# LayerNorm, S4 convolution and an NF4 gated MLP on one core: a rewritten head order, a smaller S4 transform, and the convolution's last chunk as one native matmul

## The chip, the core and the metric

The kernel runs on one core of a Trainium2 chip. The core has five engines, each with its own in-order queue: TensorE (PE in the profile; PEld is its weight load), VectorE (DVE), ScalarE (ACT), GpSimd (POOL) and SyncE (SP), which here only issues DMA transfers. The engines meet through semaphores. TensorE writes only to PSUM, the accumulator memory; the other data lie in SBUF, the on-chip memory of 128 partitions, or in DRAM. The metric is device time in microseconds (us) of one execution; lower is better.

## The reference

Input is x, four sequences of 512 rows by 512 columns, 2,048 rows in all. With xn = LayerNorm(x) over the columns, the output is

```
x + S4(xn) + MLP(xn)
S4(xn)  = causal convolution of each row of xn (512 long) with a kernel K of 512 taps, + D * xn
K       = ifft(at_roots).real, at_roots from a Cauchy sum over 64 states
MLP(xn) = (silu(xn Wg^T) * (xn Wu^T)) Wd^T,   Wg, Wu: 1792 x 512,   Wd: 512 x 1792
```

The three weights come as 4-bit codes (NF4, as int32 numbers 0 to 15) with a scale for every 64 numbers. All is float32.

## The kernel before

**Tiling.** The 2,048 rows are four blocks (tb 0 to 3) of 512; a block is four token tiles of 128 rows. The 1,792 hidden columns are 14 tiles m of 128; for each m the gate codes (k = 0) and the up codes (k = 1) form one matrix of 128 x 1024 numbers. A sum over 512 columns is four chunks of 128 (NC = 4).

**Matmuls.** Most products run as `fp32r` matmuls of three parts each: `split` and `part_of` make of a number a high part (h, on ACT), a low part (l, on DVE) and a part e (on DVE) that mends what the first two lose, with the factors LAM = 4096 and OUT = 4097. Three fp32r matmuls stand for one float32 product (`product`, L449; `conv`, L487; `down`, L514). The first matrix (m = 0) for blocks 0 and 1, the transposes, and the S4 setup use native float32 matmuls on unsplit numbers (`product_native`, L457). In the profile a native matmul makes two records, an fp32r one and a transpose make one.

**Dequantisation.** A code becomes its NF4 value by eight ACT steps in place (`bends`, L264), then DVE multiplies by the scales (`mul`, L599 in the head, L274 after it) and the parts are split off (`wp` tiles; L143 h, L145 l, L147 e).

**The head.** The string HEAD lists the work of the first three matrices and of the LayerNorm of all blocks, step by step: `stats.tb.j` (two DVE instructions for token tile j), `scale.tb.half` (two POOL instructions, add and power -0.5, for two token tiles), `norm.tb.j` (DVE), `turn.tb.half` (eight PE transposes), `copy` (ACT, turned rows to SBUF), `h`, `l`, `e` (parts of the turned rows), `bend.m.j.k.half` (bend j on 256 columns), `mul`, `w.m.part`, `native.k.tb.j.c` (two native matmuls for two token tiles and two chunks), `pass.k.m.tb.part` (four fp32r matmuls), `silu`, `gated`, and `awake.n` (n transposes of the identity, whose results nobody uses). After tracing the steps, dependencies are added that keep this order on ACT, DVE, PE and SP. GpSimd is not among them. Outside the head a scheduler orders each engine's queue by what is ready.

**After the head.** For m = 2 to 11 the loop dequantises matrix m + 1, runs `hidden` (all blocks; 24 matmuls of 128 x 512 for each), and at some m the weights of the down projection. `s4_roots` (after m = 2) forms the Cauchy sums: on PE four native matmuls into `pss` (L355), whose results DVE copies to `ss` (L360) and works on in small steps (L367 to L369). `s4_toeplitz` (after m = 3) forms K: 16 DVE steps make 128 x 128 tiles `ar` and `ai` for four residues r4, 12 native matmuls form `pm` (L421), and DVE and POOL make the Toeplitz matrix `toep`, split into `tp`. The convolution `conv(tb)` runs after m = 5 to 8: for each of four token tiles, column chunk i of the turned rows (i = 0 to 3) multiplies the first 512 - 128 i columns of `tp`, in three parts, so the matmuls are 512, 384, 256 and 128 wide. At the end `down` multiplies with Wd and adds, for each block.

Of the kernel before, what the change touches and what calls it, by code (L numbers as in the profile page):

```python
# [63 lines left out]


HEAD = """
awake.45 stats.0.0 bend.0.0.0.0 bend.0.0.0.1 bend.0.1.0.0 stats.0.1 bend.0.1.0.1
bend.0.2.0.0 stats.0.2 bend.0.2.0.1 scale.0.0 bend.0.3.0.0 bend.0.4.0.0 bend.0.3.0.1
stats.0.3 bend.0.5.0.0 bend.0.6.0.0 bend.0.4.0.1 norm.0.0 scale.0.1 bend.0.7.0.0 norm.0.1
bend.0.0.1.1 bend.0.5.0.1 mul.0.0.0 turn.0.0 awake.4 bend.0.1.1.1 norm.0.2 bend.0.6.0.1  # L70
norm.0.3 bend.0.0.1.0 bend.0.7.0.1 stats.1.0 turn.0.1 copy.0.0 mul.0.0.1 stats.1.1
bend.0.1.1.0 native.0.0.0.0 bend.0.2.1.1 bend.0.2.1.0 stats.1.3 scale.1.0 native.0.0.0.1
copy.0.1 stats.1.2 bend.0.3.1.0 native.0.0.1.0 bend.0.3.1.1 norm.1.0 scale.1.1 bend.0.4.1.0
native.0.0.1.1 bend.0.4.1.1 norm.1.1 bend.0.5.1.0 bend.0.5.1.1 norm.1.3 turn.1.0
bend.0.6.1.0 norm.1.2 bend.0.7.1.0 bend.0.6.1.1 turn.1.1 mul.0.1.0 bend.0.7.1.1 copy.1.0
mul.0.1.1 native.1.0.0.0 stats.2.0 w.0.0 native.1.0.0.1 stats.2.1 native.1.0.1.0 copy.1.1
stats.2.3 scale.2.0 native.1.1.0.0 bend.1.0 stats.2.2 native.1.0.1.1 norm.2.1 scale.2.1
silu.0.0 native.0.1.0.0 norm.2.0 bend.1.1 gated.0.0 turn.2.0 norm.2.3 norm.2.2
native.0.1.0.1 h.2.0 w.0.1 turn.2.1 bend.1.2 stats.3.0 native.0.1.1.0 bend.1.3 e.2.0
native.1.1.1.0 h.2.1 native.1.1.0.1 l.2.0 bend.1.4 native.0.1.1.1 l.2.1 native.1.1.1.1  # L80
bend.1.5 pass.1.0.2.0 e.2.1 bend.1.6 pass.1.0.2.1 w.0.2 bend.1.7 pass.0.0.2.0 silu.0.1 mul.1
pass.0.0.2.1 bend.2.0 pass.0.0.2.2 stats.3.1 w.1.0 pass.1.0.2.2 stats.3.3 scale.3.0 h.1
pass.0.1.2.0 w.1.1 pass.1.1.2.0 stats.3.2 silu.0.2 pass.0.1.2.1 norm.3.1 h.0 scale.3.1
pass.0.1.1.0 norm.3.0 gated.0.1 pass.1.1.2.1 w.1.2 bend.2.1 turn.3.0 norm.3.3 pass.1.1.2.2
h.3.0 gated.0.2 pass.0.1.2.2 norm.3.2 l.3.0 pass.1.1.1.0 silu.1.2 bend.2.2 turn.3.1
gated.1.2 load.3.0 e.3.0 pass.0.1.0.0 h.3.1 pass.1.1.0.0 bend.2.3 l.1 pass.0.1.3.0 bend.2.4
pass.1.1.3.0 bend.2.5 l.3.1 pass.0.1.1.1 bend.2.6 pass.1.1.1.1 e.3.1 pass.0.1.3.1 l.0
pass.0.0.3.0 pass.0.0.3.1 pass.0.1.3.2 e.1 pass.1.1.3.1 pass.0.0.3.2 e.0 pass.1.1.3.2
silu.0.3 bend.2.7 pass.1.0.3.0 silu.1.3 pass.1.1.1.2 mul.2 pass.1.1.0.1 gated.1.3 w.2.0
pass.0.1.0.1 w.2.1 pass.0.1.1.2 pass.1.1.0.2 silu.1.1 w.2.2 pass.0.1.0.2 gated.1.1  # L90
pass.0.2.0.0 silu.1.0 pass.1.2.0.0 pass.0.2.0.1 pass.1.2.0.1 pass.1.2.0.2 pass.0.2.0.2
pass.1.0.3.1 silu.2.0 pass.1.0.3.2 gated.0.3 gated.2.0 gated.1.0
"""


# [1 line left out]
def layernorm_s4_nf4_glu_kernel(  # L97
# [301 lines left out]
    def s4_toeplitz():  # L399
        qr, qi, nqi = roots["qr"], roots["qi"], roots["nqi"]  # L400
        b, b1 = (work.tile([P, 4, 512], F32, tag="xt", name=f"s4b{k}") for k in range(2))
        nc.sync.dma_start(b[:, 0:4, 0:256], dft)
        nc.sync.dma_start(b1[:, 0:2, :], twist)

        G.tensor_scalar(b[:, 0:4, 256:512], b[:, 0:4, 0:256], -1.0, None, ALU.mult)
        al, be, ar, ai = (b1[:, j, :] for j in range(4))
        for r4 in range(4):
            c = bass.ts(r4, P)
            o = slice(r4, r4 + 1)
            V.tensor_scalar(ar[:, c], al[:, c], qr[:, o], None, ALU.mult)  # L410
# [4 lines left out]

        pm = bank2("pm")[:, 0, :].rearrange("p (k q) -> p k q", k=4)
        for k, terms in enumerate((((0, 0),), ((2, 0),), ((1, 0), (3, 0)), ((1, 1), (3, 3)))):
            n = 2 * len(terms)
            for i, (r4, turn) in enumerate(terms):
                for part, lhsT in enumerate((ar, ai)):  # L420
                    T.matmul(  # L421
                        pm[:, k, :], lhsT[:, bass.ts(r4, P)],
                        b[:, r4, bass.ts((turn + part) % 4, P)],
                        start=(i == 0 and part == 0), stop=(2 * i + part == n - 1),
                    )
# [50 lines left out]
        gated(m, tb, ps[:, 1, :], silu(m, tb, ps[:, 0, :], OUT), OUT)  # L476


    def conv(tb, toep):
        xr = work.tile([P, 4, HD], F32, tag="xt", name=f"xr{tb}")  # L480
        nc.sync.dma_start(xr, rows(x, tb))
        for jj in range(0, 4, 2):
            po = bank2(f"pc{tb}_{jj}")
            for k in range(2):
                for i in range(NC):
                    for part in range(3):
                        T.matmul(  # L487
                            po[:, k, i * P : HD], xT[tb][part][:, jj + k, i, :],
                            toep[:, part, 0 : HD - i * P],
                            start=(i == 0 and part == 0), stop=(i == NC - 1 and part == 2),  # L490
                        )
# [252 lines left out]
```

## Time and profile before

| | us |
|---|---|
| median of 3 runs | 519.51 (519.39 to 519.62) |
| the profiled execution, its own time | 519.46 |
| its span, from first to last instruction | 517.7 |
| PE busy | 510.5 (99% of the span) |
| ACT busy | 261.6 (51%) |
| DVE busy | 260.3 (50%) |
| POOL busy | 22.1 (4%) |

The profile is one execution. Busy time of PE counts modelled ends of pipelined matmuls, so the distance between starts tells what a matmul takes from its queue. A line of the timeline has start, length, engine, source line, operation, written tile <- read tiles, shapes, count, and in brackets the idle time of the engine before it and what ended it. A line of the chain of waits in order of time has start, length, and what was waited for or ran. The view by windows gives TensorE a granted clock of 1.0 in every 2 us of the first 20; its own records begin at 5.2 us, and the `awake` transposes start every 0.213 us before that moment and every 0.109 us after it.

### The profile page before, as it was taken

How to read it: one execution, taken by the hardware profiler on the slowest of the kernel's cores; microseconds unless marked ns; L12 is line 12 of the kernel's file. 1: busy time of each engine (PE TensorE's matmuls, PEld its weight loads, DVE VectorE, ACT ScalarE, POOL GpSimd, SP SyncE). 2: the span in 40 equal slices, each digit the busy share in tenths (PEclk: the TensorE clock that was granted, in tenths of full speed). 3: DMA queues.
4: the chain of work that ended last, by engine and by line, in shares of the span. 5: the costliest groups of instructions: out<-in, count | busy, mean ns of one | idle time of the engine just before them, and what ended most of it. 6: DMA issues, size and time to landing. Idle time of an engine off the chain costs nothing.

```text
span 517.7 us, 6206 instructions
## 1 busy us (share of the span) xinstructions
PE 510.5 (99%) x2369; PEld 426.9 (82%) x2369; DVE 260.3 (50%) x352; ACT 261.6 (51%) x326; POOL 22.1 (4%) x42
## 2 busy tenths in 40 slices
PE   8999999999999999999999999999999999999996
PEld 7788888888888888888888888888888888888885
DVE  5899759935546553543522323113536536436412
ACT  7897369689999989899252202002112121121100
POOL 1310000200000000000000000121000000000000
PEclk9999999999999999999999999999999999999999
DMA  8915322796786678765845222789534524524102
GB/s 284 291 64 159 118 90 87 292 258 239 262 286 223 213 267 314 235 210 198 292 161 200 85 103 81 262 327 349 204 118 143 197 109 160 198 90 162 42 0 81
DMA packets 37085, 96.45 MB, mean 186 GB/s; under 512 B 4672, under 2 KB 5312, under 8 KB 34240
## 3 DMA queue, kind: packets, MB, share of 16 engines
q1 hardware_dynamic: 34320, 80.60, 44.9%
q0 software_dynamic: 2592, 15.21, 8.2%
q8 instruction: 18, 0.29, 0.2%
q10 hardware_dynamic: 144, 0.26, 0.1%
q14 instruction: 11, 0.09, 0.1%
HBM read 61.97 MB, written 34.08 MB: 186 GB/s over the span
## 4 chain that ended last, share of the span: by engine, by line
PE 96%; DMA 2%; SPq 1%; DVE 0%; issue 0%
PE gu L449 57%; PE po L514 30%; PE pc L487 6%; PE gu L457 2%; DMA sc_g1u<-in_gate_s_dram 2%; PE pt L204 1%; SPq L171 1%; PE pm L421 1%; SPq L250 0%; SPq L243 0%; PE pss L355 0%; DVE xo L521 0%; DVE x L192 0%
## 5 line engine op out<-in xcount | busy, mean ns | idle before, releaser
L514 PE MATMUL po<-wdt,hp 128*128 128x512 f32 x672 | 153.0, 390 | 0.0
L514 PEld LDWEIGHTS po<-wdt,hp 128*128 128x128 f32 x672 | 125.9, 188 | 27.0 <-DVE xo L521 0.9
L469 DVE SCALAR_TENSOR_TENSOR h<-gu,h 128x512 f32<-128x512 f32 x56 | 38.4, 688 | 109.4 <-ACT h L465 101.0
L143 ACT ACTIVATE hp<-hr 128x1024 fp32r<-128x1024 f32 x28 | 29.7, 1060 | 105.2 <-PE po L514 101.3
L465 ACT ACTIVATE h<-gu 128x512 f32<-128x512 f32 x56 | 33.0, 589 | 95.0 <-PE gu L449 95.0
L145 DVE TENSOR_TENSOR hp<-hr,hp 128x1024 fp32r<-128x1024 f32 x28 | 34.3, 1225 | 62.7 <-ACT hp L143 62.7
L147 DVE SCALAR_TENSOR_TENSOR hp<-hp 128x1024 fp32r<-128x1024 f32 x28 | 34.2, 1223 | 0.9
L449 PE MATMUL gu<-xhT,wp_gu 128*128 128x512 f32 x80 | 21.0, 394 | 0.0
L449 PE MATMUL gu<-xlT,wp_gu 128*128 128x512 f32 x80 | 20.7, 389 | 0.0
L487 PE MATMUL pc<-tp,xeT 128*128 128x512 f32 (+1 forms) x64 | 20.7, 323 | 0.0
L487 PE MATMUL pc<-tp,xlT 128*128 128x512 f32 (+1 forms) x64 | 20.6, 322 | 0.0
L449 PE MATMUL gu<-xeT,wp_gu 128*128 128x512 f32 x80 | 20.5, 390 | 0.0
L487 PE MATMUL pc<-tp,xhT 128*128 128x512 f32 (+1 forms) x64 | 20.3, 318 | 0.0
L521 DVE SCALAR_TENSOR_TENSOR xo<-po,xo 128x512 f32<-128x512 f32 x16 | 10.8, 688 | 18.1 <-PE po L514 18.1
L449 PEld LDWEIGHTS gu<-xlT,wp_gu 128*128 128x128 f32 x80 | 15.0, 188 | 3.1
L449 PEld LDWEIGHTS gu<-xhT,wp_gu 128*128 128x128 f32 x80 | 14.9, 188 | 3.2 <-ACT h L465 0.2
L449 PEld LDWEIGHTS gu<-xeT,wp_gu 128*128 128x128 f32 x80 | 14.9, 188 | 3.1
L457 PE MATMUL gu<-xf,q_g0u 128*128 128x256 f32 x64 | 14.6, 382 | 0.0
L457 PEld LDWEIGHTS gu<-xf,q_g0u 128*128 128x128 f32 x64 | 11.7, 190 | 1.8 <-DVE q_g0u L599 0.2
L487 PEld LDWEIGHTS pc<-tp,xhT 128*128 128x128 f32 x64 | 12.2, 190 | 0.9
L487 PEld LDWEIGHTS pc<-tp,xlT 128*128 128x128 f32 x64 | 12.0, 188 | 0.8
L487 PEld LDWEIGHTS pc<-tp,xeT 128*128 128x128 f32 x64 | 12.1, 188 | 0.6
(271 smaller groups left out, 912.1 us busy)
## 6 DMA issues: line engine op xcount, KB each, us to landing
hd<-h SPq DMA_DIRECT2D x56, 256.0 KB, 2.9
hr<-hd SPq DMA_DIRECT2D x28, 512.0 KB, 3.3
wdt<-wdd POOLq DMA_DIRECT2D x7, 1024.0 KB, 6.8
xr<-in_x_dram SPq DMA_DIRECT2D x4, 1024.0 KB, 6.8
rd<-xr SPq DMA_DIRECT2D x4, 1024.0 KB, 5.8
xo<-rd POOLq DMA_DIRECT2D x4, 1024.0 KB, 5.9
out_dram<-xo SPq DMA_DIRECT2D x16, 256.0 KB, 3.5
wdt<-wdd POOLq DMA_DIRECT2D x7, 512.0 KB, 7.3
```

Source lines behind the costliest of these rows:

```text
L143: S.activation(dst[0], src, AF.Copy, scale=TRIM)
L145: V.tensor_tensor(dst[1], src, f(dst[0]), ALU.subtract)
L147: V.scalar_tensor_tensor(dst[2], f(dst[1]), -LAM, f(dst[0]), ALU.mult, ALU.add)
L171: nc.sync.dma_start(xs[tb][:, j : j + step, :], rows(x, tb)[:, j : j + step, :])
L204: T.transpose(pt[:, i, bass.ts(c, P)], xs[tb][:, jj + i, bass.ts(c, P)], ident)
L449: T.matmul(ps[:, k, :], wp[:, part, k, bass.ts(c, P)], xT[tb][part][:, :, c, :], start=(part == 0 and c == 0), stop=(part == 2 and c == NC ...
L457: T.matmul(ps[:, k, j.start * P : j.stop * P], w[:, k, bass.ts(c, P)], xf[tb].rearrange("p j (c q) -> p j c q", c=NC)[:, j, c, :], start=( ...
L465: S.activation(h, pg, AF.Silu, scale=unit)
L469: V.scalar_tensor_tensor(h, pu, unit, h, ALU.mult, ALU.mult)
L487: T.matmul(po[:, k, i * P : HD], xT[tb][part][:, jj + k, i, :], toep[:, part, 0 : HD - i * P], start=(i == 0 and part == 0), stop=(i == NC ...
L514: T.matmul(po[j], hp[:, part, k, bass.ts(j, P)], wd(p, part, k), start=(p == 0 and k == 0 and part == 0), stop=(p == NPR - 1 and k == 1 an ...
L521: V.scalar_tensor_tensor(o, po[j], OUT, o, ALU.mult, ALU.add)
```

## The change

Three things are changed. First, HEAD is another list, and GpSimd is added to the engines on which it is kept. In the new list the code bends of the first matrix alternate between its two halves, `scale` steps stand directly behind their statistics, block 0 instead of block 1 is split first of these two, and the last steps of the three matrices stand in another order. The first lines of the list before:

```diff
-awake.45 stats.0.0 bend.0.0.0.0 bend.0.0.0.1 bend.0.1.0.0 stats.0.1 bend.0.1.0.1
-bend.0.2.0.0 stats.0.2 bend.0.2.0.1 scale.0.0 bend.0.3.0.0 bend.0.4.0.0 bend.0.3.0.1
-stats.0.3 bend.0.5.0.0 bend.0.6.0.0 bend.0.4.0.1 norm.0.0 scale.0.1 bend.0.7.0.0 norm.0.1
-bend.0.0.1.1 bend.0.5.0.1 mul.0.0.0 turn.0.0 awake.4 bend.0.1.1.1 norm.0.2 bend.0.6.0.1
-norm.0.3 bend.0.0.1.0 bend.0.7.0.1 stats.1.0 turn.0.1 copy.0.0 mul.0.0.1 stats.1.1
-bend.0.1.1.0 native.0.0.0.0 bend.0.2.1.1 bend.0.2.1.0 stats.1.3 scale.1.0 native.0.0.0.1
-copy.0.1 stats.1.2 bend.0.3.1.0 native.0.0.1.0 bend.0.3.1.1 norm.1.0 scale.1.1 bend.0.4.1.0
-native.0.0.1.1 bend.0.4.1.1 norm.1.1 bend.0.5.1.0 bend.0.5.1.1 norm.1.3 turn.1.0
-bend.0.6.1.0 norm.1.2 bend.0.7.1.0 bend.0.6.1.1 turn.1.1 mul.0.1.0 bend.0.7.1.1 copy.1.0
-mul.0.1.1 native.1.0.0.0 stats.2.0 w.0.0 native.1.0.0.1 stats.2.1 native.1.0.1.0 copy.1.1
...
-pass.0.1.0.1 w.2.1 pass.0.1.1.2 pass.1.1.0.2 silu.1.1 w.2.2 pass.0.1.0.2 gated.1.1
-pass.0.2.0.0 silu.1.0 pass.1.2.0.0 pass.0.2.0.1 pass.1.2.0.1 pass.1.2.0.2 pass.0.2.0.2
-pass.1.0.3.1 silu.2.0 pass.1.0.3.2 gated.0.3 gated.2.0 gated.1.0
```

and now:

```diff
+awake.43 stats.0.0 bend.0.0.0.0 bend.0.0.0.1 bend.0.1.0.0 stats.0.1 bend.0.1.0.1
+bend.0.2.0.0 bend.0.2.0.1 stats.0.2 scale.0.0 bend.0.3.0.0 bend.0.3.0.1 stats.0.3
+bend.0.4.0.0 bend.0.4.0.1 bend.0.5.0.0 norm.0.0 scale.0.1 bend.0.0.1.0 bend.0.5.0.1 norm.0.1
+bend.0.6.0.0 turn.0.0 awake.3 bend.0.6.0.1 norm.0.3 bend.0.1.1.0 bend.0.7.0.0 norm.0.2
+bend.0.7.0.1 stats.1.1 turn.0.1 copy.0.0 mul.0.0.0 bend.0.2.1.0 mul.0.0.1 native.0.0.0.0
+bend.0.0.1.1 stats.1.0 bend.0.3.1.0 copy.0.1 native.0.0.0.1 stats.1.3 scale.1.0 bend.0.4.1.0
+native.0.0.1.0 stats.1.2 bend.0.1.1.1 bend.0.5.1.0 bend.0.2.1.1 native.0.0.1.1 norm.1.1
+scale.1.1 bend.0.6.1.0 norm.1.0 bend.0.3.1.1 bend.0.7.1.0 turn.1.0 bend.0.4.1.1 mul.0.1.0
+bend.0.5.1.1 norm.1.3 native.1.0.0.0 bend.0.6.1.1 norm.1.2 bend.0.7.1.1 silu.0.0 turn.1.1
+mul.0.1.1 copy.1.0 native.1.0.1.0 stats.2.2 copy.1.1 stats.2.3 native.0.1.0.0 stats.2.0
...
+silu.1.3 pass.0.1.1.2 w.2.2 pass.1.1.1.2 gated.1.3 pass.1.0.3.1 pass.0.2.0.0 pass.0.0.3.2
+pass.0.2.0.1 silu.0.3 silu.1.1 pass.1.0.3.2 pass.1.2.0.0 gated.0.3 gated.1.1 pass.1.2.0.1
+pass.0.2.0.2 pass.1.2.0.2 silu.2.0 gated.2.0
```

Second, the S4 transform: the term of residue 3 is the mirrored conjugate of that of residue 1, so the host arranges the constants (`_layouts`) so that `s4_toeplitz` adds the fourth residue's `ar` and `ai` onto the second's, and `pm` needs eight matmuls; the cosine table loses a quarter.

Third, the last chunk of the convolution: `last_chunk(tb)` joins the high and low part of a block's last column chunk to whole float32 numbers in a buffer of its own (tag "xn", two buffers), `tn` holds the first 128 columns of `toep` divided by OUT, and one native matmul of 128 x 128 takes the place of three fp32r ones of that width.

```diff
ident = const.tile([P, P], F32, tag="ident", name="ident")
     make_identity(nc, ident)
     tp = const.tile([P, 3, L], F32R, tag="tp", name="tp")
+    tn = const.tile([P, P], F32, tag="tn", name="tn")
     const.tile([P, 16], F32, tag="fill", name="fill")
 
 
@@ -399,30 +401,38 @@
     def s4_toeplitz():
         qr, qi, nqi = roots["qr"], roots["qi"], roots["nqi"]
         b, b1 = (work.tile([P, 4, 512], F32, tag="xt", name=f"s4b{k}") for k in range(2))
-        nc.sync.dma_start(b[:, 0:4, 0:256], dft)
+        nc.sync.dma_start(b[:, 0:3, 0:256], dft)
         nc.sync.dma_start(b1[:, 0:2, :], twist)
 
-        G.tensor_scalar(b[:, 0:4, 256:512], b[:, 0:4, 0:256], -1.0, None, ALU.mult)
+        G.tensor_scalar(b[:, 0:3, 256:512], b[:, 0:3, 0:256], -1.0, None, ALU.mult)
         al, be, ar, ai = (b1[:, j, :] for j in range(4))
+
+
         for r4 in range(4):
+            to = bass.ts((0, 1, 2, 1)[r4], P)
             c = bass.ts(r4, P)
             o = slice(r4, r4 + 1)
-            V.tensor_scalar(ar[:, c], al[:, c], qr[:, o], None, ALU.mult)
-            V.scalar_tensor_tensor(ar[:, c], be[:, c], nqi[:, o], ar[:, c], ALU.mult, ALU.add)
-            V.tensor_scalar(ai[:, c], al[:, c], qi[:, o], None, ALU.mult)
-            V.scalar_tensor_tensor(ai[:, c], be[:, c], qr[:, o], ai[:, c], ALU.mult, ALU.add)
+            for dst, s1, s2 in (
+                ((ar, qr, nqi), (ai, qi, qr)) if r4 < 3 else ((ar, qr, qi), (ai, nqi, qr))
+            ):
+                if r4 < 3:
+                    V.tensor_scalar(dst[:, to], al[:, c], s1[:, o], None, ALU.mult)
+                else:
+                    V.scalar_tensor_tensor(
+                        dst[:, to], al[:, c], s1[:, o], dst[:, to], ALU.mult, ALU.add
+                    )
+                V.scalar_tensor_tensor(
+                    dst[:, to], be[:, c], s2[:, o], dst[:, to], ALU.mult, ALU.add
+                )
 
 
         pm = bank2("pm")[:, 0, :].rearrange("p (k q) -> p k q", k=4)
-        for k, terms in enumerate((((0, 0),), ((2, 0),), ((1, 0), (3, 0)), ((1, 1), (3, 3)))):
-            n = 2 * len(terms)
-            for i, (r4, turn) in enumerate(terms):
-                for part, lhsT in enumerate((ar, ai)):
-                    T.matmul(
-                        pm[:, k, :], lhsT[:, bass.ts(r4, P)],
-                        b[:, r4, bass.ts((turn + part) % 4, P)],
-                        start=(i == 0 and part == 0), stop=(2 * i + part == n - 1),
-                    )
+        for k, (r4, turn) in enumerate(((0, 0), (2, 0), (1, 0), (1, 1))):
+            for part, lhsT in enumerate((ar, ai)):
+                T.matmul(
+                    pm[:, k, :], lhsT[:, bass.ts(r4, P)], b[:, r4, bass.ts(turn + part, P)],
+                    start=(part == 0), stop=(part == 1),
+                )
         toep = work.tile([P, L], F32, tag="h", name="toep", bufs=4)
         tk = toep.rearrange("p (k q) -> p k q", k=4)
         cd = b1[:, 0, 0:384].rearrange("p (k q) -> p k q", k=3)
@@ -440,6 +450,7 @@
             toep[:, 0:P], ident, row[:, 64:65], toep[:, 0:P], ALU.mult, ALU.add
         )
         split([tp[:, i, :] for i in range(3)], toep)
+        S.activation(tn, toep[:, 0:P], AF.Copy, scale=1.0 / OUT)
         return tp
 
 
@@ -476,19 +487,32 @@
         gated(m, tb, ps[:, 1, :], silu(m, tb, ps[:, 0, :], OUT), OUT)
 
 
+
+
+    whole = {}
+
+    def last_chunk(tb):
+        whole[tb] = work.tile([P, 4, P], F32, tag="xn", name=f"xn{tb}")
+        h, low = (f(xT[tb][i][:, :, NC - 1, :]) for i in range(2))
+        V.scalar_tensor_tensor(whole[tb], h, LAM, low, ALU.mult, ALU.add)
+
     def conv(tb, toep):
         xr = work.tile([P, 4, HD], F32, tag="xt", name=f"xr{tb}")
         nc.sync.dma_start(xr, rows(x, tb))
         for jj in range(0, 4, 2):
             po = bank2(f"pc{tb}_{jj}")
             for k in range(2):
-                for i in range(NC):
+                for i in range(NC - 1):
                     for part in range(3):
                         T.matmul(
                             po[:, k, i * P : HD], xT[tb][part][:, jj + k, i, :],
                             toep[:, part, 0 : HD - i * P],
-                            start=(i == 0 and part == 0), stop=(i == NC - 1 and part == 2),
+                            start=(i == 0 and part == 0), stop=False,
                         )
+                T.matmul(
+                    po[:, k, (NC - 1) * P : HD], whole[tb][:, jj + k, :], tn,
+                    start=False, stop=True,
+                )
             o = xr[:, jj : jj + 2, :]
             V.scalar_tensor_tensor(o, po, OUT, o, ALU.mult, ALU.add)
         nc.sync.dma_start(res_dram[tb], xr)
@@ -628,13 +652,15 @@
         qs.pop(gu(m))
     last = {}
     order = mybir.DependencyInfo(mybir.DependencyClass.NoSync, mybir.DependencyReason.DATA)
-    ordered = (S.engine, V.engine, T.engine, sp.engine)
+    ordered = (S.engine, V.engine, T.engine, G.engine, sp.engine)
     end = len(traced)
     for ins in list(traced[start:end]):
         if ins.engine in last and ins.engine in ordered:
             tc.add_manual_dep(ins, last[ins.engine].name, order, reason="order of the first tiles")
         last[ins.engine] = ins
     for m in range(2, NMT - 2):
+        if 5 <= m < 9:
+            last_chunk(m - 5)
         wp[m + 1] = dequant(gu(m + 1))
         for tb in range(1 if m == 2 else 0, NTB):
             hidden(m, tb, wp[m])
@@ -699,9 +725,12 @@
     row = [np.asarray(a[f"L0_attn_{n}"]).reshape(-1) for n in ("Bp", "D", "log_step")]
 
     lr = 4 * np.arange(P)[:, None] + np.arange(4)[None, :]
+    lr[:, 3] = lr[::-1, 3]
     half = np.pi * lr / L
     th = 2 * np.pi * ((lr[:, :, None] * np.arange(P)) % L) / L
     tw = np.pi * ((lr[:, :, None] * (1 - 2 * np.arange(P))) % (2 * L)) / L
+    tw = np.stack([np.cos(tw), np.sin(tw)], axis=1) / L
+    tw[:, 1, 3] *= -1.0
     f = np.float32
     return {
         "x": np.asarray(a["L0_attn_u"]).reshape(NTOK, HD),
@@ -715,8 +744,8 @@
         "s4_row": np.concatenate(row)[None, :],
         "trig": np.stack([np.sin(half), np.cos(half)]).transpose(0, 2, 1).reshape(2, L).astype(f),
         "cos_col": np.cos(half).astype(f),
-        "dft": np.concatenate([np.cos(th), -np.sin(th)], axis=2).astype(f),
-        "twist": (np.stack([np.cos(tw), np.sin(tw)], axis=1) / L).reshape(P, 2, 512).astype(f),
+        "dft": np.concatenate([np.cos(th), -np.sin(th)], axis=2)[:, :3].astype(f),
+        "twist": tw.reshape(P, 2, 512).astype(f),
     }
```

More of the change, by code (lines that the diff above doesn't have):

```diff
@@ L73 @@
-copy.0.1 stats.1.2 bend.0.3.1.0 native.0.0.1.0 bend.0.3.1.1 norm.1.0 scale.1.1 bend.0.4.1.0
-native.0.0.1.1 bend.0.4.1.1 norm.1.1 bend.0.5.1.0 bend.0.5.1.1 norm.1.3 turn.1.0
-bend.0.6.1.0 norm.1.2 bend.0.7.1.0 bend.0.6.1.1 turn.1.1 mul.0.1.0 bend.0.7.1.1 copy.1.0
-mul.0.1.1 native.1.0.0.0 stats.2.0 w.0.0 native.1.0.0.1 stats.2.1 native.1.0.1.0 copy.1.1
-stats.2.3 scale.2.0 native.1.1.0.0 bend.1.0 stats.2.2 native.1.0.1.1 norm.2.1 scale.2.1
-silu.0.0 native.0.1.0.0 norm.2.0 bend.1.1 gated.0.0 turn.2.0 norm.2.3 norm.2.2
@@ L79 @@
[L79 to L89, printed above, removed]
-pass.0.1.0.1 w.2.1 pass.0.1.1.2 pass.1.1.0.2 silu.1.1 w.2.2 pass.0.1.0.2 gated.1.1
@@ new lines @@
+native.1.0.0.1 w.0.0 scale.2.1 stats.2.1 native.0.1.0.1 bend.1.0 norm.2.3 scale.2.0
+native.1.0.1.1 bend.1.1 w.0.1 native.1.1.0.0 bend.1.2 norm.2.0 native.0.1.1.0 norm.2.1
+bend.1.3 gated.0.0 turn.2.0 norm.2.2 native.1.1.0.1 h.2.0 w.0.2 turn.2.1 bend.1.4 e.2.0
+native.0.1.1.1 h.2.1 native.1.1.1.0 l.2.0 bend.1.5 native.1.1.1.1 stats.3.1 silu.0.1
+pass.1.0.2.0 l.2.1 bend.1.6 pass.0.0.2.0 bend.1.7 e.2.1 pass.0.0.2.1 pass.1.0.2.1 mul.1
+pass.0.0.2.2 stats.3.3 w.1.0 pass.1.0.2.2 stats.3.0 h.0 pass.0.1.2.0 w.1.1 scale.3.0
@@ new lines @@
+pass.1.1.2.0 gated.0.1 bend.2.0 pass.0.1.2.1 w.1.2 silu.0.2 pass.1.1.2.1 h.1 l.0
+pass.0.1.0.0 pass.1.1.0.0 bend.2.1 pass.1.1.2.2 stats.3.2 bend.2.2 pass.0.1.2.2 norm.3.1
+scale.3.1 norm.3.0 pass.0.1.0.1 silu.1.2 e.0 bend.2.3 pass.1.1.0.1 turn.3.0 norm.3.3
+pass.0.1.0.2 h.3.0 gated.0.2 pass.1.1.0.2 norm.3.2 gated.1.2 load.3.0 turn.3.1 silu.1.0
+e.3.0 pass.0.1.1.0 h.3.1 gated.1.0 pass.1.1.1.0 bend.2.4 l.3.0 pass.0.1.3.0 bend.2.5 l.3.1
+pass.1.1.3.0 bend.2.6 pass.0.0.3.0 e.3.1 bend.2.7 pass.0.1.3.1 l.1 pass.1.1.3.1 pass.1.0.3.0
@@ L93 @@
+pass.0.0.3.1 mul.2 pass.0.1.1.1 e.1 w.2.0 pass.0.1.3.2 pass.1.1.3.2 w.2.1 pass.1.1.1.1
+silu.1.3 pass.0.1.1.2 w.2.2 pass.1.1.1.2 gated.1.3 pass.1.0.3.1 pass.0.2.0.0 pass.0.0.3.2
+pass.0.2.0.1 silu.0.3 silu.1.1 pass.1.0.3.2 pass.1.2.0.0 gated.0.3 gated.1.1 pass.1.2.0.1
+pass.0.2.0.2 pass.1.2.0.2 silu.2.0 gated.2.0
 """
```

## The prediction

> **What bounds the kernel now.** I read the page first, for the busy shares and the chain of waits by line.
>
> ```profile
> PE 510.5 (99%) x2369; PEld 426.9 (82%) x2369; DVE 260.3 (50%) x352; ACT 261.6 (51%) x326; POOL 22.1 (4%) x42
> ...
> PE 96%; DMA 2%; SPq 1%; DVE 0%; issue 0%
> ```
>
> TensorE carries the chain. The chain in order of time says from where on:
>
> ```profile
> 8.79 7.84 DMA sc_g1u<-in_gate_s_dram
> ...
> 16.66 0.55 DVE x L192
> ...
> 17.26 1.09 PE pt L204 x8
> ...
> 360.80 152.88 PE po L514 x672
> ```
>
> The columns are start, length and what. From 17.26 us to 513.68 every piece but one "issue" of 0.00 us is PE's. So the time is the moment at which PE stops waiting in the head, plus all matmuls after it, plus a 0.69 us DVE tail. A step is worth what it takes off PE's queue, or what it moves that moment; DVE, ACT and POOL count only where PE waits for them.
>
> **The convolution's last chunk.** PE's timeline in the first conv:
>
> ```profile
> 157.41 0.22 PE L487 MATMUL pc<-tp,xhT 128*128 128x128 f32 x1
> 157.47 0.28 PE L487 MATMUL pc<-tp,xlT 128*128 128x128 f32 x1
> 157.58 0.27 PE L487 MATMUL pc<-tp,xeT 128*128 128x128 f32 x1
> 157.69 0.44 PE L487 MATMUL pc<-tp,xhT 128*128 128x512 f32 x1
> 157.97 0.40 PE L487 MATMUL pc<-tp,xlT 128*128 128x512 f32 x1
> ```
>
> Read starts, not durations, since matmuls overlap. A 512-wide matmul steps 0.227 us (21.82 us for 96 in the chain). From the first 128-wide start to the second 512-wide one are 0.56 us; less 0.227, the three 128-wide ones take 0.333. One native matmul of the same size replaces them. Its price is in the S4 transform:
>
> ```profile
> 109.62 2.84 PE L421 MATMUL pm<-s4b,s4b 128*128 128x128 f32 x24
> 112.22 0.71 PE L449 MATMUL gu<-xhT,wp_g4u 128*128 128x512 f32 x2
> ```
>
> These 24 records are 12 native matmuls (two records each). From 109.62 to 112.53, the start of the second matmul after them, less 0.227, gives 2.68, so 0.2235 each, the change of kind at both ends included. Saved: 0.333 - 0.2235 = 0.11, taken as 0.106 because a lone native matmul pays both changes itself; 16 times (4 blocks x 4 token tiles): **-1.70 us**. [...]
>
> The joins (L469's kind of row, 128x512 scalar_tensor_tensor, 0.69 us, stepping 0.60) are four on DVE, a 128x128 copy (0.3 us at most) is one on ACT. In the built program two joins stand inside the head's DVE queue, after the low part of block 0 and after the low part of block 1. I cost them at nothing. Cover: DVE is busy 50%; walking the head's queues with the rows' durations, the passes behind the first join still find their operands 0.45 us early. Without that cover each costs 0.6 us, 1.2 in all. The join of blocks 2 and 3 shares two buffers with 0 and 1, but a conv lies 29 us after the one before, and by then the older buffer is read.
>
> **The S4 transform.** Eight matmuls instead of 12: 4 x 0.2235 = **-0.89 us**, in PE's queue with no wait before it in the trace. DVE still issues 16 small steps; two become 0.35 instead of 0.28. POOL's negation and the DMA shrink by a quarter. All lie ahead of pm by over 4 us (DVE's last s4b step ends at 104.9, pm starts at 109.62).
>
> **The head.** What PE waits for last is in DVE's timeline:
>
> ```profile
> 11.09 0.69 DVE L181 BATCH_NORM_STATS2 st<-x 128x6 f32<-128x512 f32 x1 [0.27 <-DMA x<-in_x_dram]
> ...
> 11.91 0.39 DVE L599 TENSOR_TENSOR q_g0u<-q_g0u,sc_g0u 128x256 f32<-128x256 f32 x1
> 12.22 0.69 DVE L181 BATCH_NORM_STATS2 st<-x 128x6 f32<-128x512 f32 x1
> ...
> 14.63 0.97 DVE L192 TENSOR_SCALAR x<-x,mv,rstd 128x512 f32<-128x512 f32 x2
> 16.20 1.00 DVE L192 TENSOR_SCALAR x<-x,mv,rstd 128x512 f32<-128x512 f32 x2 [0.60 <-POOL rstd L187]
> ```
>
> Before, PE had done eight native matmuls and turned half of block 1 when it waited 0.95 us for rows 2 and 3 of block 1 (16.20 + 1.00 -> 17.26). Take out the eight transposes (0.87): the equivalent moment "native eight done, block 1 not turned, no waiting from here" is 17.26 - 0.87 = 16.39.
>
> After, DVE's queue from the landing of block 1 (11.06, same DMA order) reads: stats, mul, mul, stats, stats, stats, norm, norm. Four stats pairs (0.82, 0.82, 0.80, 0.79) and two muls (0.32 each): 11.09 + 3.23 + 0.65 = 14.97; two norms 0.97: 15.94, and one 0.06 to PE: 16.0. Is PE free? The first mul now stands behind a stats that waits for the DMA: it ends 12.30 instead of 9.90, so native starts at 12.35 (before 11.43) and eight of 0.434 (0.87 for the four records at 24.41 in the chain) end at 15.82. Its other inputs come sooner: ACT's interleaved bends finish the first half at about 10.4 and the copy of the first turned rows at 11.6. PE waits 0.2 us for the norm and then goes on: **-0.35 us** (16.03 against 16.39). Rows 2 and 3 then: aggregate at about 15.07, plus the 1.49 from aggregate to norm that POOL took before (14.71 -> 16.20), plus 1.0, at PE 17.6; PE comes at 16.0 + 0.87 + 0.87 = 17.77. That margin of 0.17 is the smallest; the others to the head's end, walked the same way, are 0.4 us or more. SP issues all loads of the first three matrices and the four blocks in the old order; only stores and later loads change places, and in the walk no engine of the head waits for one. The first transposes start earlier (POOL now finishes each half's power in order, norm 0 at 7.46 instead of 8.57) and two awake steps go with 45 -> 43 and 4 -> 3; worth nothing, as PE waits later anyway.
>
> PE stands idle for some 1.8 us before 12.35, the longest stop after the warm-up. In the trace stops of 0.95 and 0.79 us left the granted clock at 1.0 and the transposes at 0.109 us. [...]
>
> **Behind the head.** Two things lie where matrix 3 (wp_g3u) starts, in PE's timeline and in DVE's:
>
> ```profile
> 86.80 1.06 PE L355 MATMUL pss<-vv,s4a 128*128 128x8 f32 x8
> 87.72 1.19 PE L449 MATMUL gu<-xhT,wp_g3u 128*128 128x512 f32 x4
> ```
> ```profile
> 86.06 0.69 DVE L351 SCALAR_TENSOR_TENSOR s4a<-s4a,s4a 64x512 f32<-64x512 f32 x1
> 86.78 1.23 DVE L145 TENSOR_TENSOR wp_g3u<-q_g3u,wp_g3u 128x1024 fp32r<-128x1024 f32 x1
> ...
> 93.06 0.18 DVE L360 COPY ss<-pss 128x32 f32<-128x32 f32 x1
> ```
>
> Before, pss waited for L351: 0.389 us from the matmul before it instead of 0.227. In the new DVE order that step ends some 2.8 us ahead: **-0.16 us**. But the new order also puts the copy of pss, and two 0.08 us steps, ahead of the l part of wp_g3u (L145's row), which PE needs. With P the start of pss: pss ends P+1.06, the copy starts P+1.10, the l part starts P+1.47 and reaches PE at P+2.75. PE is through pss and six matmuls at P+0.91+1.48 = P+2.39: **+0.36 us** of new waiting. Queued behind the waiting copy are also the gating of the last block and the e part; the e part comes 0.07 early.
>
> **Sum.** -1.70 - 0.89 - 0.35 - 0.16 + 0.36 = -2.74, on the profiled execution's own 519.46 us (span 517.7 plus 1.76 around it; the median is 519.51): 516.7 us.
>
> **The rivals.**
>
> 1. Slower: a lone native matmul inside the fp32r stream is not hidden as in a run of 12. Bound from the rows: both weight loads (0.188) and both matmuls (0.275) in full, 0.93 instead of 0.333: +9.5 us in conv, 527.9 in all. The other terms gain 1.04, so it is slower from 0.40 us each on, and measurably from 0.46. Against: L457's native pairs between transposes at 24.24 take 0.87 for two, and pm's edges cost nothing visible. Chance 4%.
>
> 2. The clock falls to half in the stop before 12.35. The warm-up took 1.41 to 5.23; 3.8 us of half speed cost 1.9 less the 0.2 of cover: 518.4. Against: the rows above. 5%.
>
> 3. The head's cover is thinner: the joins show, or block 1 lands later, up to 1.2 us: 517.9. For: margins of 0.17 and 0.45. 10%.
>
> 4. The 0.36 is not there, or PE waits less before 16.03 (0.2): 516.1. 12%.
>
> The forecast has the remaining 69%.
>
> **How the numbers follow.** The range from 516.1 (rival 4) to 518.0 (rival 3) leaves out rival 1, most of 2 and some error of the rows. Faster by over 0.2% (1.04 us, about what a measurement of this kernel can tell from no change) is below 518.5: the forecast, 3 and 4, 0.91; within, rival 2, which lies on that bound, 0.05; slower, rival 1, 0.04.
>
> **What would show it.** Right: 0.22 us per native in conv (a conv of about 7.2 us, not 7.62, in the chain); pm 1.8 us; the first transposes of block 1 at 16.0 and no PE wait up to pss; a wait of 0.3 to 0.5 us of PE for the l part of wp_g3u behind pss. Wrong: conv at or over 7.6 us, native records in the head stepping 0.43 us instead of 0.217, or a PE wait between 17 and 86 us.

## The result, and the profile after

The changed kernel takes 516.84 us (median; 516.40 to 519.29) against 519.51 (519.01 to 520.45) for the kernel before: ratio 0.9951, interval 0.994 to 0.9963. The profiled execution takes 516.43 us, span 514.7, so it is 3.03 us below the profiled execution of before.

The page after, busy time and then the chain's shares by engine:

```profile
PE 507.2 (99%) x2342; PEld 423.7 (82%) x2342; DVE 261.8 (51%) x356; ACT 261.6 (51%) x327; POOL 25.7 (5%) x42
...
PE 97%; DMA 1%; ACT 1%; SPq 1%; DVE 0%; issue 0%
```

TensorE still sets the end; what changed is its own queue. The chain in order of time, after (start, length, what):

```profile
12.13 3.69 PE gu L468 x16
15.83 1.00 PE pt L206 x8
...
86.07 0.81 PE pss L357 x8
...
87.35 1.15 DVE wp_g3u L147
88.50 0.04 issue
88.54 20.72 PE gu L460 x90
109.26 1.78 PE pm L432 x16
...
241.66 1.57 PE pc L507 x9
243.23 0.22 PE pc L512 x2
...
248.88 108.85 PE gu L460 x480
357.73 152.90 PE po L538 x672
```

From 12.13 to the last DVE step the chain leaves PE only once, at `pss`. `pm` is 1.78 (2.68 before), a convolution is 241.66 to 248.88, 7.22 (7.62 before), and each lone native matmul (L512, two records) stands in it with 0.22. PE's timeline around the first of them:

```profile
155.99 0.38 PE L512 MATMUL pc<-tn,xn 128*128 128x128 f32 x2
156.13 0.48 PE L507 MATMUL pc<-tp,xhT 128*128 128x512 f32 x1
156.44 0.40 PE L507 MATMUL pc<-tp,xlT 128*128 128x512 f32 x1
```

Further up, PE's timeline shows the new wait, in brackets, and the start of `pm`:

```profile
85.91 0.95 PE L357 MATMUL pss<-vv,s4a 128*128 128x8 f32 x8
86.71 1.65 PE L460 MATMUL gu<-xhT,wp_g3u 128*128 128x512 f32 x6
88.54 1.20 PE L460 MATMUL gu<-xlT,wp_g3u 128*128 128x512 f32 x4 [0.18 <-DVE wp_g3u L147]
...
109.10 1.95 PE L432 MATMUL pm<-s4b,s4b 128*128 128x128 f32 x16
```

The six h matmuls start at 86.71 and the l matmuls at 88.54, 1.83 later; six steps take 1.48. DVE's timeline has the cause:

```profile
86.89 0.19 DVE L362 COPY ss<-pss 128x32 f32<-128x32 f32 x1 [1.35 <-PE pss L357]
87.12 0.16 DVE L369 TENSOR_TENSOR dr<-ss,ccol 128x4 f32<-128x4 f32 x1
87.20 0.15 DVE L369 TENSOR_TENSOR di<-ss,ccol 128x4 f32<-128x4 f32 x1
87.27 1.22 DVE L147 TENSOR_TENSOR wp_g3u<-q_g3u,wp_g3u 128x1024 fp32r<-128x1024 f32 x1
```

DVE idled 1.35 us until `pss` was ready for the copy, with the l part queued behind that copy.

### The profile page after: what moved, and what is told of

It reads as the page before. It is cut to its first block, busy times and chain, and to the rows that moved or that the text cites. A ratio compares the mean times of both kernels' runs of the same rounds, so it can differ in the third digit from the quotient of the medians.

```text
span 514.7 us, 6164 instructions
## 1 busy us (share of the span) xinstructions
PE 507.2 (99%) x2342; PEld 423.7 (82%) x2342; DVE 261.8 (51%) x356; ACT 261.6 (51%) x327; POOL 25.7 (5%) x42
## 4 chain that ended last, share of the span: by engine, by line
PE 97%; DMA 1%; ACT 1%; SPq 1%; DVE 0%; issue 0%
PE gu L460 57%; PE po L538 30%; PE pc L507 5%; PE gu L468 3%; PE pt L206 1%; DMA q_g0u<-in_up_q_dram 1%; PE pc L512 1%; ACT q_g0u L266 1%; PE pm L432 0%; SPq L173 0%; DVE wp_g3u L147 0%; SPq L252 0%; ACT xf L212 0%; PE pss L357 0%; DVE xo L545 0%
## 5 line engine op out<-in xcount | busy, mean ns | idle before, releaser
L507 PE MATMUL pc<-tp,xhT 128*128 128x512 f32 (+2 forms) x48 | 17.2, 358 | 0.0
L507 PE MATMUL pc<-tp,xeT 128*128 128x512 f32 (+2 forms) x48 | 16.3, 340 | 0.0
L507 PE MATMUL pc<-tp,xlT 128*128 128x512 f32 (+2 forms) x48 | 16.1, 336 | 0.0
L529 POOL DMA_DIRECT2D xo<-rd x4 | 2.4, 590 | 218.8 <-DVE q_d10d L276 109.3
L517 DVE SCALAR_TENSOR_TENSOR xr<-pc,xr 128x1024 f32<-128x1024 f32 x8 | 9.8, 1221 | 6.1 <-PE pc L512 6.1
L183 DVE BATCH_NORM_STATS2 st<-x 128x6 f32<-128x512 f32 x16 | 10.8, 675 | 3.8 <-DMA x<-in_x_dram 3.7
```

The source lines that it names most:

```text
L183: V.bn_stats(st[:, j, :], xs[tb][:, j, :])
L507: T.matmul(po[:, k, i * P : HD], xT[tb][part][:, jj + k, i, :], toep[:, part, 0 : HD - i * P], start=(i == 0 and part == 0), stop=False,)
```

## The experiments

The theory: the gain is matmuls taken off PE's queue, conv and `pm`; the head list gives some tenths and takes about as much back at `pss`. The rivals: one of the two edits brings nothing or all, or the head decides.

**The conv edit alone.** The kernel before with `tn`, `last_chunk` and the native matmul:

```diff
-                for i in range(NC):
+                for i in range(NC - 1):
...
+                T.matmul(
+                    po[:, k, (NC - 1) * P : HD], whole[tb][:, jj + k, :], tn,
+                    start=False, stop=True,
+                )
```

> The kernel before with the third edit alone (joins, tn and one native matmul for the last chunk), old head and old S4 transform. Theory (each edit is worth what it takes off PE's queue): a conv of 7.2 us instead of 7.62 in the chain, four times, so 1.6 to 1.7 us less, 517.8 by the median, with no PE wait at the two joins that stand in the old head's DVE queue. Rival one (the gain of the whole change comes from the head, the lone native matmul pays its own cost back): conv at 7.6 us, 519.5. Rival two (the joins show in the head): conv at 7.2 us, but new PE waits of 0.6 to 1.2 us before 66 us, 518.5 to 519.

Measured: 518.01 (517.63 to 518.92) against 519.78 on the same chip, ratio 0.9969 [0.9958, 0.998]: -1.77 us. The prediction's term was -1.70. In its profile the stretch from the first convolution to the end of the fourth takes 94.30 us (95.93 before), 1.63 less, and from 17.64 us to that point the chain never leaves PE, so no join shows.

**The S4 transform alone.**

```diff
+                if r4 < 3:
+                    V.tensor_scalar(dst[:, to], al[:, c], s1[:, o], None, ALU.mult)
+                else:
+                    V.scalar_tensor_tensor(
+                        dst[:, to], al[:, c], s1[:, o], dst[:, to], ALU.mult, ALU.add
+                    )
```

> The kernel before with the second edit alone (S4 transform on added conjugate terms, eight matmuls into pm). Theory: pm takes 1.78 us instead of 2.68, 0.9 us less, 518.6. Rival (pm is covered by something else that PE must wait for, such as the next matrix's parts): PE waits up to 0.9 us behind pm and the time stays at 519.5.

Measured: 518.64 (518.21 to 519.29), ratio 0.9979 [0.9971, 0.9988]: -1.14, with `pm` at 1.78 in its chain. The chain says -0.90; the medians leave room for 0.24 of other things.

**The head alone.** The new list, and GpSimd kept in order:

```diff
-    ordered = (S.engine, V.engine, T.engine, sp.engine)
+    ordered = (S.engine, V.engine, T.engine, G.engine, sp.engine)
```

> The kernel before with the first edit alone (new head list, GpSimd kept in order). Theory: PE goes on without a wait from 15.8 to 16.0 us at the first transposes of block 1 (worth 0.35 to 0.6), pss doesn't wait (0.16), and PE waits 0.36 us for the l part of matrix 3 behind the copy of pss, since the scheduler puts that copy early under this head list: 0.2 to 0.4 us less in all, 519.2. Rival (the head is where the change gains): 2 us less, 517.5.

Measured: 520.15 (519.36 to 522.37), ratio 1.0014 [1.0002, 1.0026]. A miss: no gain, and a wider spread than that of the kernel before (519.03 to 520.50 on the same chip). PE's timeline in its profile:

```profile
12.49 3.69 PE L457 MATMUL gu<-xf,q_g0u 128*128 128x256 f32 x16 [1.27 <-ACT q_g0u L264]
16.13 1.07 PE L204 MATMUL pt<-ident,x 128*128 128x128 f32 x8
17.03 1.03 PE L457 MATMUL gu<-xf,q_g0u 128*128 128x256 f32 x4
18.07 1.07 PE L204 MATMUL pt<-ident,x 128*128 128x128 f32 x8
...
89.10 1.19 PE L449 MATMUL gu<-xlT,wp_g3u 128*128 128x512 f32 x4 [0.20 <-DVE wp_g3u L145]
```

This execution ran at a clock of 1.0 and took 519.70, 0.24 more than the profile of before. Two things cost here. The wait at `pss` comes with the list alone: from matrix 3's first matmul to `pm` are 22.57 us, 0.67 more than before, where the prediction had 0.36. And four native records take 0.87, so the transposes at 18.07 could have begun at 17.90: PE waited 0.17 for rows 2 and 3 of block 1, since POOL's power took 1.19 us in this execution (0.86 in the profile of the changed kernel). That was the prediction's smallest margin; with it used up, PE is only 0.05 us ahead of before at that point. The stretch from there to matrix 3 is 0.41 shorter. The spread is taken up below.

**The copy of `pss` behind the parts of matrix 3.** The changed kernel with one order added:

```diff
+        if pair == (("g", 3), ("u", 3)):
+            wp3.append([i for i in nc.cur_bb.bb.instructions if i.engine == V.engine][-1])
...
         V.tensor_copy(ss, pss)
+        tc.add_manual_dep(
+            [i for i in nc.cur_bb.bb.instructions if i.engine == V.engine][-1], wp3[0].name,
...
```

> The changed kernel with one order dependency more: DVE's copy of pss stands behind the last part of matrix 3. Theory: the 0.35 us of PE waiting for the l part at 88 us goes and nothing takes its place, as the roots are not needed before the transform some 15 us later: 0.35 us less than the changed kernel, 516.1 if that is 516.5. Rival (another wait is just behind, the e part or the h part of matrix 3, or the S4 steps come late for pm): the same time as the changed kernel, with a PE wait at 88 to 91 us or ahead of pm.

Measured: 516.63 (515.60 to 518.93), ratio 0.9944 [0.9926, 0.9962]; the profiled execution 515.92, 0.51 below that of the changed kernel, with block 1 landing at the same moment (10.71 and 10.70 us). Its chain:

```profile
86.08 0.79 PE pss L360 x8
86.87 21.90 PE gu L468 x96
108.76 1.78 PE pm L440 x16
```

No wait is left, and `pm` starts 0.50 earlier with `pss` where it was. So the wait's price is 0.50: the 0.35 of the gap, and the rest in slower steps after it. By the medians (0.2 us) it can't be told from nothing.

**Without `awake`.** The changed kernel without its 46 warm-up transposes.

```diff
-awake.43 stats.0.0 bend.0.0.0.0 bend.0.0.0.1 bend.0.1.0.0 stats.0.1 bend.0.1.0.1
+stats.0.0 bend.0.0.0.0 bend.0.0.0.1 bend.0.1.0.0 stats.0.1 bend.0.1.0.1
...
-bend.0.6.0.0 turn.0.0 awake.3 bend.0.6.0.1 norm.0.3 bend.0.1.1.0 bend.0.7.0.0 norm.0.2
+bend.0.6.0.0 turn.0.0 bend.0.6.0.1 norm.0.3 bend.0.1.1.0 bend.0.7.0.0 norm.0.2
```

> The changed kernel without its awake steps (43 and 3 transposes of the identity). Theory (transposes count for the clock, and the warm-up in the stop before the data is what they are for): with no work before 8.2 us the transposes step 0.213 us and some of the native matmuls step 0.43 instead of 0.217, until the clock rises some 3 to 4 us after the start; 1.5 to 2.5 us more than the changed kernel, 518 to 519. [...]

Measured: 517.73 (516.50 to 519.77), ratio 0.9965 [0.9948, 0.9981] on another chip than the runs above: below the theory's 518 to 519, and 0.89 above the changed kernel's median of 516.84. PE's timeline:

```profile
8.37 3.84 PE L206 MATMUL pt<-ident,x 128*128 128x128 f32 x16 [8.37 <-DVE x L194]
12.69 3.69 PE L468 MATMUL gu<-xf,q_g0u 128*128 128x256 f32 x16 [0.48 <-ACT q_g0u L266]
```

The transposes run slower (sixteen take 3.84 us; in the changed kernel eight take 1.11 and 1.09), and the natives behind them take 3.69, as with `awake`: they ran at full speed from 12.69 on, with nothing but transposes run on PE before. In this execution the slow transposes cost nothing, for they end 0.48 us before PE has its next operands: it took 517.00, 0.57 more than the profile of the changed kernel, and block 1's statistics on DVE, which set the natives' start (see below), began 0.56 later. What the three slowest runs (518.58 to 519.77) lost is not shown. None was profiled, and the view by windows gives a clock of 1.0 over the slow transposes too (10 to 11 us in this profile), so a mean clock tells nothing of a late rise.

**Fillers in the stop, and both together.** First the changed kernel with more `awake` behind each half of block 0, then the same with the copy of `pss` moved as above. The theory: the late runs of the new head, those at a clock of 0.995 to 0.997 (up to 2.89 us above the lowest run of the changed kernel), are the clock falling in these stops. If so, an estimate from these runs is that with the stops filled the highest run comes within 1 us of the lowest and the median falls by 0.2 to 0.5.

```diff
-bend.0.6.0.0 turn.0.0 awake.3 bend.0.6.0.1 norm.0.3 bend.0.1.1.0 bend.0.7.0.0 norm.0.2
+bend.0.6.0.0 turn.0.0 awake.9 bend.0.6.0.1 norm.0.3 bend.0.1.1.0 bend.0.7.0.0 norm.0.2
-bend.0.7.0.1 stats.1.1 turn.0.1 copy.0.0 mul.0.0.0 bend.0.2.1.0 mul.0.0.1 native.0.0.0.0
+bend.0.7.0.1 stats.1.1 turn.0.1 awake.8 copy.0.0 mul.0.0.0 bend.0.2.1.0 mul.0.0.1 native.0.0.0.0
```

> The changed kernel with more awake steps in the two stops of the new head: 9 instead of 3 behind the first turned half of block 0, and 8 new ones behind the second, so that TensorE stops 0.1 and 0.3 us instead of 0.62 and 0.79 to 1.3. [...]

> The changed kernel with the filled stops of the run before and with DVE's copy of pss behind the last part of matrix 3. Theory: lowest run 515.6 as with the copy alone, highest within 1 us of it, median 516.0, below both kernels. Rival: median 516.6 and a spread of 3 us as without the filling.

Measured: 517.19 (516.54 to 517.32), ratio 0.9944 [0.9932, 0.9956], and 516.61 (516.36 to 517.77), 0.994 [0.9928, 0.9952]. The medians are those of the changed kernel within their intervals. The spread is smaller, as the theory has it (the highest of these ten runs is 517.77, and none has a mean clock below 0.998), though ten runs are few for that; neither median fell as it expected, the second not to 516.0. With the copy moved, the profile shows another margin gone: DVE's e part took 1.87 us (1.21 with the copy alone moved) and PE's e matmuls came 0.31 late.

**Each join twice.**

```diff
-        V.scalar_tensor_tensor(whole[tb], h, LAM, low, ALU.mult, ALU.add)
+        for _ in range(2):
+            V.scalar_tensor_tensor(whole[tb], h, LAM, low, ALU.mult, ALU.add)
```

> The changed kernel with each of the four joins issued twice (the same numbers written again). Theory (the joins are covered by DVE's idle time): no new PE wait, the same time. Rival (the two joins in the head's DVE queue show): up to 0.6 us each, 1.2 us more, as PE waits before 66 us.

Measured: 517.61 (516.79 to 517.95), ratio 0.9953 [0.994, 0.9966]. PE's chain is without a break from its natives at 13.47 us to `pss`, and the 168 matmuls ahead of `pss` take 38.25 us there and 38.13 in the changed kernel, so the joins are covered even twice but for 0.12 us at most. The natives began 1.34 us later than in the profile of the changed kernel, which the joins can't cause: the first stands behind them.

**What the head hangs on.** The late start explains itself from DVE's timeline. The changed kernel, and then the one with the joins doubled:

```profile
10.70 0.69 DVE L183 BATCH_NORM_STATS2 st<-x 128x6 f32<-128x512 f32 x1 [0.50 <-DMA x<-in_x_dram]
11.43 0.18 DVE L184 BATCH_NORM_AGGREGATE mv<-st 128x2 f32<-128x6 f32 x1
11.61 0.76 DVE L623 TENSOR_TENSOR q_g0u<-q_g0u,sc_g0u 128x256 f32<-128x256 f32 x2
```
```profile
12.04 0.69 DVE L183 BATCH_NORM_STATS2 st<-x 128x6 f32<-128x512 f32 x1 [1.41 <-DMA x<-in_x_dram]
...
12.95 0.76 DVE L624 TENSOR_TENSOR q_g0u<-q_g0u,sc_g0u 128x256 f32<-128x256 f32 x2
```

The first scale multiplication stands behind statistics that wait for block 1. Call their start S. In PE's timeline of the changed kernel S is followed by:

```profile
12.13 3.69 PE L468 MATMUL gu<-xf,q_g0u 128*128 128x256 f32 x16 [0.79 <-ACT q_g0u L266]
15.77 1.06 PE L206 MATMUL pt<-ident,x 128*128 128x128 f32 x8
16.67 1.03 PE L468 MATMUL gu<-xf,q_g0u 128*128 128x256 f32 x4
17.53 1.04 PE L206 MATMUL pt<-ident,x 128*128 128x128 f32 x8
```

In the seven profiles with the new list so far, S is 10.70, 10.71, 11.06, 11.26, 11.53, 12.04 and 12.04, and the first native starts at S + 1.43 in every one (12.13 to 13.47). The bracket names a code bend on ACT, which ended up to 0.49 us earlier; the constant distance from S says that the multiplication is what the native waits for. In the old list the natives start as early as 11.43, but rows 2 and 3 of block 1 are turned at S + 6.16 or 6.17 in all four of its profiles, the last below included (in two of them S is set by DVE's own queue, not by the landing). In the new list that is S + 6.82 or 6.83 in four profiles and S + 6.95 to 7.01 in the three where DVE waited 0.60 us for POOL (the head alone among them), with four native records (0.86) already done: S + 5.97, or 6.09 to 6.15. So the new list's own gain is 0.20 us, 0.02 to 0.08 where POOL was late, and the landing of block 1 (S from 10.70 to 12.04) moves the start by up to 1.3 us.

**The scale multiplications first.** With the copy of `pss` moved, `mul.0.0.0 mul.0.0.1` go ahead of `stats.1.1`, and the gate codes' bends ahead of the up codes':

```diff
-bend.0.7.0.1 stats.1.1 turn.0.1 copy.0.0 mul.0.0.0 bend.0.2.1.0 mul.0.0.1 native.0.0.0.0
+bend.0.7.0.1 turn.0.1 copy.0.0 mul.0.0.0 mul.0.0.1 stats.1.1 bend.0.0.1.0 native.0.0.0.0
```

> The copy of pss stays behind the parts of matrix 3. In the head the two scale multiplications of the gate codes stand ahead of block 1's statistics on DVE, and the gate codes' last bends ahead of the up codes' on ACT. Theory (in all profiles of the new head the native matmuls start 1.43 us after block 1's statistics, its first transposes 5.07 us after them, and so the whole queue of PE follows the landing of block 1): the natives start at about 11.1 us whenever block 1 lands, its first transposes 4.3 to 4.4 us after the statistics start, unless the up codes' scales come later; 0.4 to 0.7 us less than with the copy moved alone (516.6): 516.0 to 516.2, and a smaller spread. Rival (the spread is the clock, or the head is set by the second norm): 516.6, spread as before.

Measured: 516.42 (516.01 to 517.53), ratio 0.9943 [0.9931, 0.9956]: lowest median of all, but above the 516.0 to 516.2 expected and not to be told from the copy alone or the changed kernel. Its profile, of the slowest of the five runs, shows the native start untied (12.56 with S at 11.83), and something else, in PE's timeline and in the view by windows (window; length, PE busy, granted clock, DMA share, GB/s):

```profile
8.86 1.11 PE L206 MATMUL pt<-ident,x 128*128 128x128 f32 x8 [1.16 <-DVE x L194]
...
10.92 1.85 PE L206 MATMUL pt<-ident,x 128*128 128x128 f32 x8 [0.62 <-DVE x L194]
12.56 4.58 PE L476 MATMUL gu<-xf,q_g0u 128*128 128x256 f32 x16
```
```profile
10.00:11.00 1.00, 0.38 (x4) 1.00 1.00 367
11.00:12.00 1.00, 1.00 (x6) 0.54 1.04 401
12.00:13.00 1.00, 1.00 (x6) 0.50 1.07 418
13.00:14.00 1.00, 1.00 (x4) 0.50 1.03 399
14.00:15.00 1.00, 1.00 (x5) 0.75 1.06 408
```

The clock fell to half at about 11 us, after idle times of 1.16 and 0.62, and stayed there for 3.4 us; transposes and natives took 0.76 and 0.89 longer. The mean granted clock of this execution is 0.997.

**A longer stop, empty and filled.** In the changed kernel the statistics of one token tile are formed five times ahead of the scale multiplications; in the second kernel 36 transposes fill the stop (the diff is of the second; the first is without `awake.36`).

```diff
-bend.0.7.0.1 stats.1.1 turn.0.1 copy.0.0 mul.0.0.0 bend.0.2.1.0 mul.0.0.1 native.0.0.0.0
+bend.0.7.0.1 stats.1.1 stats.1.1 stats.1.1 stats.1.1 stats.1.1 turn.0.1 awake.36 copy.0.0 mul.0.0.0 bend.0.2.1.0 mul.0.0.1 native.0.0.0.0
```

> The changed kernel with the statistics of one token tile of block 1 formed five times instead of once ahead of the scale multiplications: four more pairs of 0.82 us on DVE, so PE's stop before the first native matmuls grows by 3.28 us to 4 or 5. If a stop costs only itself: 516.8 + 3.3 = 520.1, the natives at 3.69 us for 16 records and a granted clock of 1.0 after it. If the stop takes the clock (the theory on the late runs of the new head): natives at twice that for some 2 to 4 us, 521.5 to 522.5, in some or all executions.

> The same four more pairs, and 36 transposes of the identity in the stop (3.9 us at 0.109). If a stop costs only itself: 520.1 again, as without them. If the stop takes the clock: 520.1 here, and 1.5 to 2.4 us more without the transposes, in some or all executions.

Measured: 522.83 (522.21 to 524.09), ratio 1.0061 [1.0047, 1.0075], without the filling, and 520.75 (520.40 to 521.82), 1.0022 [1.0013, 1.0031], with it. PE needs the same work in both, and 2.08 us lie between them. PE's timelines, empty and filled, and the clock of the empty one by windows (window; length, PE busy, granted clock, DMA share, GB/s):

```profile
16.85 6.72 PE L468 MATMUL gu<-xf,q_g0u 128*128 128x256 f32 x16 [4.95 <-ACT q_g0u L266]
```
```profile
16.86 3.69 PE L468 MATMUL gu<-xf,q_g0u 128*128 128x256 f32 x16 [1.55 <-ACT q_g0u L266]
```

```profile
14.00:16.00 2.00, 0.00 (x0) 1.00 1.07 362
16.00:18.00 2.00, 1.15 (x3) 0.54 1.09 255
...
22.00:24.00 2.00, 2.00 (x11) 0.76 0.10 31
```

The natives start at the same moment and take 6.72 or 3.69. In the profile the clock fell to half late in the stop of 4.95 us, at about 16.2 by the windows, and stayed there for 6.8 us. The mean clock says the same of all five executions (0.991 or 0.992), and with transposes in the stop of none of ten (0.998 to 1.0). The filled kernel's profile still has a stop of 1.55 us, and its clock stayed at 1.0.

**The old head with both other edits.** The changed kernel with the list of before and without GpSimd in the order.

> The changed kernel with the head list of the kernel before and without GpSimd in the kept order: the conv and transform edits alone, together. If the parts add up (-1.77 and -1.14 by the medians, -1.60 and -0.90 by the chains): 516.9 to 517.2, so the new head is worth nothing by the median. If the new head is worth the predicted 0.35 + 0.16 - 0.36: 0.15 us more than the changed kernel.

Measured: 517.58 (516.65 to 518.19), ratio 0.996 [0.9947, 0.9972]. The medians of the two single edits add up to -2.91, this one shows -2.08, less than either expectation, and the whole change -2.67: the intervals overlap, and the medians don't settle on which side of nothing the new head lies. The profile does better. Block 1's statistics start at 11.91 there, 0.82 later than in the profile of before; 0.82 - 0.90 - 1.63 is -1.71, and its own time is 517.69, 1.77 below before.

## Why the prediction was right

It said 516.7 (516.1 to 518.0), faster; the median is 516.84. Its steps against the profile, each from starts on PE's timeline or pieces of the chain:

| step | predicted | profiled |
|---|---|---|
| conv, from the first to the end of the fourth | -1.70 | -1.63 (156.00 to 251.93 before, 154.58 to 248.88 now) |
| `pm` | -0.89 | -0.90 |
| head, up to block 1's rows 2 and 3 | -0.35 | -0.59 |
| from there to matrix 3's first matmul | -0.16 | -0.42 |
| from there to `pm` | +0.36 | +0.49 |
| sum | -2.74 | -3.05 (own times: -3.03) |

- **Conv.** From the native's start (155.99) to the second matmul after it (156.44), less 0.227 for one 512-wide step, are 0.22 us, the price taken from `pm`. The change of kind at both ends cost nothing beyond it, and rival 1 is out. Alone the edit gave 1.77, so the trace's rows (0.333 for the three fp32r matmuls, 0.2235 for a native one) were the right price.
- **`pm`.** As worked out.
- **Head.** The prediction took block 1 to land when it had landed before. In the profile after it landed 0.39 earlier (S 10.70 for 11.09), which is luck of this execution, and the list's own part is 0.20. (The prediction's rows add up to 16.00 and -0.39, where it wrote 16.03 and -0.35.) The mis-sized terms: natives start at S + 1.43 (predicted S + 1.26), and their eight take 3.64 to the next transposes (predicted 3.47), so PE did not wait for the norm; it came later than it.
- **Up to matrix 3.** The wait of 0.16 before `pss` is gone, `pss` itself takes 0.80 to the next matmul instead of 0.92, and 0.14 is not assigned; of these 0.42 the prediction had only the wait.
- **The new wait.** 0.35 for 0.36, at the place and for the reason given; slower steps behind it make it 0.49. The copy moved behind shows it whole: 0.50.
- **The joins.** Covered, also when doubled, but for 0.12 us.
- **The sum.** Conv and `pm` came as worked out, in size and in cause. The other terms make -0.52 in the profile where the prediction had -0.15, 0.39 of it the landing, and the median stands 0.41 above the profiled execution. So that the median is within 0.15 of 516.7 is in part luck.
- **Rival 2, the clock, was set aside too firmly.** That the stops of before left the clock at 1.0 was one execution's answer. In the changed kernel two of nine runs have a mean clock below 0.998, and they are the two highest: 517.60 at 0.997 and 519.29 at 0.995; without them the median would be 516.66. (A mean of 0.998 says nothing of the head: in the changed kernel's profile the clock is below 1.0 only behind the last matmul, at half from 513 us on.) With the head alone four of twelve are below, 520.68 to 522.37; the seven with 0.999 or more have a median of 519.70, which is 0.08 below the kernel before. So the miss of the head alone has two parts: the gain that its profile does not show even at a clock of 1.0, and runs with a lower clock. That the clock falls in the head is shown in one profile (0.997) and by the longer stop; the runs at 0.995 were not profiled, and for them it is argued from their clock alone. It comes more often with the new list, but not with it alone: below 0.998 are eight of its 54 runs, the long stops left out, and two of 73 with the old list whose clock is on record (519.29 at 0.995 for the transform alone, 0.65 above its median, and 520.52 at 0.997 for the kernel before).
- **Rival 3** happened in part. Its thinner margin cost 0.17 in the head alone, and its later landing is in two profiles of the new list (S 12.04, 0.95 later than before; 517.95 with the joins doubled); in the profile of the changed kernel the landing fell the other way. **Rival 4** came true as far as PE did not wait for the norm.

What stays open: the value of the new head in the median, and a version that beats the changed kernel measurably. The copy moved, the scales first and the fillers give 516.42 to 517.19, all inside the changed kernel's interval.

## What to carry to other kernels

Price each edit on the queue of the bounding engine by starts in the trace, and compare profiles only after taking out when their inputs landed: here one transfer moved the start by up to 1.3 us, more than the head edit's own gain in the head (0.20). A step that waits for a transfer should not stand in front of a step that the bounding engine needs sooner (moving it untied the start in the profile; its worth in the median is not shown). And a gap on TensorE can cost more than its length, as the stop of 4.95 us did (2.1 us on top), so fill a long one; with the short ones filled no median fell here. Look at the granted clock of all runs, not only at the profile's.

## What the runs showed of the hardware

- In a stop of 4.95 us on PE the clock fell to half and was there for 6.8 us in the profile, and the mean clock of all five executions agrees. Of shorter stops, 1.16 and 0.62 us were followed by 3.4 us at half in one profiled execution (scales first), while longer ones left the clock at 1.0: 1.27 (head alone), 1.55 (long stop filled) and 1.69, with 0.62 shortly before it (joins twice). So in these profiles the length of a stop does not decide alone; which short stop brings the half clock is not settled.
- With 36 transposes of the identity in the stop, ten of ten executions have a mean clock of 0.998 or more; without them, five of five have 0.991 or 0.992. Without `awake`, PE ran sixteen transposes and nothing else before its first natives, and these took 3.69 us for 16 records, as with `awake`.
- POOL's power on 128 x 2 for the second half of block 1 took 0.86 us in nine of the fourteen profiles and 1.19 or 1.20 in five; why is not shown.
